# Another order inside a unit of the second attention, parameter rows by GpSimd's queue, the last row tile quantised in halves

## The chip, the cores and the metric

The kernel runs on one core of one Trainium2 chip. The time is the device time of one execution in microseconds (us); of three runs the median is shown. The core has five engines with a queue of instructions each: TensorE (PE in the profile, its weight loads are PEld), VectorE (DVE), ScalarE (ACT), GpSimd (POOL) and SyncE (SP), which here only issues DMAs. Instructions of one engine run in the order of the program; between engines they wait for semaphores.

## The reference

Two transformer blocks, one after the other, over x of 4 batches x 1024 rows x 512 features, with a condition vector of 512 for each batch:

```python
# block 1
tp = gelu(time_emb) @ Wt + bt;  scale, shift = split(tp, 2)
h = layer_norm(x, ln1_g, ln1_b) * (1 + scale) + shift
q, k, v = split_heads(h @ Wqkv)                    # 16 heads of 32
scores = q @ k.T / sqrt(32) - torus_dist * torus_scale   # padded keys to -1e30
x = x + (softmax(scores) @ v) @ Wout
x = x + (gelu(layer_norm(x, ln2_g, ln2_b) @ W1 + b1) @ W2 + b2)
# block 2: bitlinear(x, w, b) = act_quant(x) @ ternary(w).T + b
xn = rmsnorm(x, g1) * (1 + scale1) + shift1        # scale1, shift1 = bitlinear(c, w_ada1)
q, k, v = split_heads(bitlinear(xn, w_qkv, b_qkv))
x = x + bitlinear(softmax(q @ k.T / sqrt(32)) @ v, w_proj, b_proj)
xn = rmsnorm(x, g2) * (1 + scale2) + shift2
x = x + bitlinear(gelu(bitlinear(xn, w_fc1, b_fc1)), w_fc2, b_fc2)   # 2048 hidden
```

`act_quant` rounds each row to integers of -128 to 127 by its largest absolute value.

## The kernel before

The program runs in five stages: the start (some 36 us: parameters, the condition's product with Wt, the norm of the first rows), the first attention, the first feed-forward part (up to about 2398 us), the second attention (2398 to 3640 us), and the last feed-forward part.

**The attention** (`attention`, from line 252) is one function for both blocks. It goes through units. A unit is 128 query rows of one group of four heads: (batch, head group, chunk of 256 queries, which half of the chunk), so there are 128 units, even ones with the first half of a chunk, odd ones with the second. Units are staggered: while the scores of unit i are made, the exponentials of unit i-1 are finished and turned, and the products of an older chunk are made. Each unit has two halves, c = 0 and 1, by the keys 0 to 511 and 512 to 1023. In a half:

- `scores` (L296): four matmuls, one per head, into four PSUM banks.
- `half` (L1364): VectorE reads the scores of each head out of PSUM into `e`, with a running least value (four half reads). `Order.reads` says for each head after how many turns its read is written.
- `turn` (L319, L322): four times per half, one head's exponentials of 512 keys of the unit before are transposed by TensorE in four 128 x 128 pieces into a bank, and copied out to `pt`. `Order.evict` names the copying engine of each turn: A is ScalarE, D is VectorE.
- `weigh` (L480): ScalarE's exponential of one head over 1024 keys; two per half. In half 0 they are those of heads 2 and 3 of the old unit, in half 1 those of heads 0 and 1 of the new one. `Order.exps` says after which turn each is written.
- `product` (L331): in odd units only, the 16 matmuls of each half that multiply `pt` of an older chunk by v; `take` copies the sums out, and `back` (L353, L357) turns them back and scales them, in even units.
- pieces: other work, spread over the slots of the units. A slot is one turn; `Order.even` and `Order.odd` name the slots (0 to 3 in half 0, 4 to 7 in half 1) that take pieces. Here they are the qkv product of the next head group (L1338, L1343, L1346, and its transposes L1354, L1355), quantising and turning the next batch's rows (L197 to L200, L830, L853, L854), and the projection of the batch before (L1282, L1287, L1288). Units that have several kinds of them, as 34 to 39, are called heavy here, those with qkv pieces alone, as 42 to 47, quiet.

The order of all this is written out by hand (`manual_schedule`), so the order of each engine's instructions is that of the program text. In the second attention scores, turns and pieces share seven PSUM banks (L1304, tag "mm"); a new tile takes the bank that the program has freed longest ago, and its first matmul waits until that bank's last reader is done.

**The start** (L499 to L622). SP loads the condition c, four row tiles x in one DMA, the second half of Wt, then the other four row tiles; ScalarE's queue loads the first half of Wt and then, in `load_vectors` (L145), six parameter vectors as rows (`vrows`) and `tscale`. ScalarE's gelu of c (L553) follows in its queue. VectorE measures and norms the rows (L559 to L567). TensorE turns the vectors (v_ps, L579), VectorE copies them out as columns (L580). TensorE makes tp4 (L584, 32 matmuls), VectorE copies it (tpr, L589), TensorE turns it (L592), VectorE adds the bias and makes mod_a and mod_b (L596 to L609). With these ScalarE writes hT (L487), which the first qkv matmuls read (L680).

**The end** (L1377 to L1516). The last part goes through 32 row tiles in a pipeline with a step for each tile (L1498): `hidden` (first product, VectorE L1446, gelu L1450), `hidden_quantised` (VectorE finds the largest value, L1455; `factors` makes the scale, L205 to L208; GpSimd scales and rounds in two passes, L1458 and L1460), `hidden_turned` (16 transposes L1469, ScalarE copies L1472), `second` (16 matmuls, L1479), `stored` (VectorE scales and adds the residual, L1488; GpSimd adds the bias b2, L1489; SP writes out, L1490).

Of the kernel before, what the change touches and what calls it, by code (L numbers as in the profile page):

```python
# [30 lines left out]
F32 = mybir.dt.float32  # L31
BF16 = mybir.dt.bfloat16
U8 = mybir.dt.uint8
AF = mybir.ActivationFunctionType
ALU = mybir.AluOpType
AX = mybir.AxisListType
# [3 lines left out]
P = 128  # L40
B, L, D, H, F = 4, 1024, 512, 16, 2048
HD = D // H
KT = D // P
FT = F // P
FH = FT // 2
LT = L // P
NT = B * LT
# [10 lines left out]
MAGIC = 12582912.0  # L58
# [16 lines left out]
    (((0, 0), (0, 1), (1, 0), (1, 1)), ((2, 0), (3, 0), (2, 1), (3, 1))), (0, 0, 0, 0),  # L75
)
ORDER_L1 = Order(
    ("AADA", "AAAD"), ((1, 2), (2, 2)), 0, (1, 0), (2, 3, 4, 7), (2, 3, 6, 7),
    (((0, 0), (0, 1), (1, 0), (1, 1)), ((2, 1), (3, 0), (2, 0), (3, 1))), (0, 0, 0, 2),
)  # L80


def two_blocks(tc: tile.TileContext, a: dict, out: bass.AP):

    nc = tc.nc
    with tc.tile_pool(name="flag", bufs=1) as pool:
        pairs = pool.tile([1, B * L // 2], mybir.dt.uint16, name="pairs")
        nc.sync.dma_start(
            pairs[:, :].bitcast(U8), a["mask"].rearrange("b l -> (b l)").unsqueeze(0)
        )  # L90
        least = pool.tile([1, 1], mybir.dt.int32, name="least")
        nc.vector.tensor_reduce(least, pairs, AX.X, ALU.min)
        whole = nc.values_load(
            least, min_val=0, max_val=ALL_VALID, skip_runtime_bounds_check_because="bytes are 0 or 1"
        )
    with tc.If(whole == ALL_VALID) as cond:
        program(tc, a, out, masked_keys=False)
    with cond.Else():
        program(tc, a, out, masked_keys=True)
# [3 lines left out]
def program(ctx: ExitStack, tc: tile.TileContext, a: dict, out: bass.AP, masked_keys: bool):  # L103
    nc = tc.nc
# [4 lines left out]
    def row(pool, name, parts=P, tag=None):  # L109

        v = a[name]
        t = pool.tile([parts, v.shape[0]], F32, name=f"row_{name}", tag=tag or f"row_{name}")
        nc.scalar.dma_start(t, v.partition_broadcast(parts))
        return t


    ident = const.tile([P, P], F32, name="ident")
# [17 lines left out]
    nv = sum(vectors.values())  # L135
    vrows = const.tile([nv, P], F32, name="vrows")
    vcols = const.tile([P, nv], F32, name="vcols")
    tscale = const.tile([P, H], F32, name="tscale")
    columns, at = [], 0
# [5 lines left out]
    def load_vectors():  # L145
        at = 0
        for name, n in vectors.items():
            nc.scalar.dma_start(vrows[at : at + n, :], a[name].rearrange("(t p) -> t p", p=P))
            at += n
        nc.scalar.dma_start(tscale, a["L0_cond_torus_scale"].partition_broadcast(P))  # L150


    mod_a = const.tile([P, KT, B], F32, name="mod_a")
# [18 lines left out]
    def copy(i, o, x):  # L172

        if i % 2:
            nc.vector.tensor_copy(o, x)
        else:
            nc.scalar.copy(o, x)
# [24 lines left out]
    def factors(small, am, wmean, deq):  # L202

        n = am.shape[0]
        nc.vector.tensor_scalar(am, am, EPS, 1.0 / 127.0, ALU.max, ALU.mult)  # L205
        s = small.tile([n, 1], F32, name="qs")
        nc.vector.reciprocal(s, am)
        nc.vector.tensor_scalar_mul(deq, am, wmean[:n])  # L208
        return s
# [283 lines left out]
    with ExitStack() as st:  # L493
# [15 lines left out]
        small = st.enter_context(tc.tile_pool(name="l0small", bufs=4))  # L509
        ps_s = st.enter_context(tc.tile_pool(name="l0ps_s", bufs=4, space=PSUM))  # L510
        ps_mm = st.enter_context(tc.tile_pool(name="l0ps_mm", bufs=3, space=PSUM))
# [4 lines left out]
        with tc.tile_pool(name="mod", bufs=1) as ap, tc.manual_schedule(engines=ALL):  # L516
# [6 lines left out]
            xs = [x0[:, t, :] for t in range(4)]  # L523
# [12 lines left out]
            load_wt(nc.scalar, 0)  # L536
            load_wt(nc.sync, 1)
            load_vectors()
            xs += [load_x(0, t) for t in range(4, LT)]

# [31 lines left out]
            def rows_normed(c):  # L572
                for t in range(4 * c, 4 * c + 4):
                    measure(t)
                normed(range(4 * c, 4 * c + 4))

            rows_normed(0)
            v_ps = ps_mm.tile([P, nv], F32, name="v_ps", tag="mm")
            nc.tensor.transpose(v_ps, vrows, ident[:nv, :nv])  # L579
            nc.vector.tensor_copy(vcols, v_ps)  # L580
            tp4 = ps_mm.tile([P, TQ], F32, name="tp4", tag="mm")
            for k in range(KT):
                for j in range(4):
# [2 lines left out]
                        rhs=wt[:, k, bass.ts(j, TQ)], start=(k == 0), stop=(k == KT - 1),  # L586
                    )
            tpr = ap.tile([P, TQ], F32, name="tpr")
            nc.vector.tensor_copy(tpr, tp4)  # L589
            tp_ps = ps_mm.tile([P, TQ // P, 4, 32], F32, name="tp_ps", tag="mm")  # L590
            for n in range(TQ // P):
                nc.tensor.transpose(  # L592
# [231 lines left out]
    means = {n: w1p.tile([P, 1], F32, name=f"mean_{n}") for n in ("q", "p", "a1", "a2", 1, 2)}  # L824
# [68 lines left out]
    with ExitStack() as st:  # L893
# [11 lines left out]
        small = st.enter_context(tc.tile_pool(name="f0small", bufs=2))  # L905
        ps_mm = st.enter_context(tc.tile_pool(name="f0ps", bufs=2, space=PSUM))
        ps_p = st.enter_context(tc.tile_pool(name="f0ps_p", bufs=2, space=PSUM))
        b2r = row(wp, "L0_cond_b2")
# [154 lines left out]
        def part(name, bufs=2):  # L1063
            return cp.tile([P, 2, TC], F32, name=name, bufs=bufs)
# [63 lines left out]
        def block(xs, moving, steps, more):  # L1128
# [31 lines left out]
            a_lo, a_hi = xs[0][:, :, :TC], xs[0][:, :, TC:]  # L1160
            b_lo, b_hi = xs[1][:, :, :TC], xs[1][:, :, TC:]
            p = second(1, "x")
            s = part("s", 1)
            nc.scalar.copy(s, p)
            nc.gpsimd.tensor_tensor(a_lo, a_lo, s, ALU.add)
            p = second(2, "y")
            nc.vector.tensor_tensor(a_lo, p, a_lo, ALU.add)
            p = second(6, "w")
            u = part("y")
            nc.vector.tensor_tensor(u, p, s, ALU.add)  # L1170
# [77 lines left out]
    small = st.enter_context(tc.tile_pool(name="a1small", bufs=4))  # L1248
# [4 lines left out]
    def row_scale3(b, n):  # L1253

        at = slice(b * LT, (b + n) * LT)
        nc.scalar.activation(rms3[:, at], squares[:, at], AF.Sqrt, bias=eps_rms, scale=1.0 / D)
        nc.vector.reciprocal(rms3[:, at], rms3[:, at])
# [40 lines left out]
    with ExitStack() as inner:  # L1298
# [5 lines left out]
        ps_mm = inner.enter_context(tc.tile_pool(name="a1ps_mm", bufs=7, space=PSUM))  # L1304
# [77 lines left out]
    with ExitStack() as inner:  # L1382
        wp = inner.enter_context(tc.tile_pool(name="f1w", bufs=1))
        b1r = row(wp, "L1_cond_b_fc1")
        b2r = row(wp, "L1_cond_b_fc2")
        magic = wp.tile([P, 1], F32, name="magic")
        nc.gpsimd.memset(magic, MAGIC)
        small = inner.enter_context(tc.tile_pool(name="f1small", bufs=6))
# [5 lines left out]
        fp = inner.enter_context(tc.tile_pool(name="f1t", bufs=3))  # L1394
        xfp = inner.enter_context(tc.tile_pool(name="f1x", bufs=LT + 2))
        rows, xs, xns, xqs, xqTs, hs, hqs, hqTs, outs = {}, {}, {}, {}, {}, {}, {}, {}, {}
        HALF = F // 2
# [54 lines left out]
        def hidden_quantised(t):  # L1452
# [7 lines left out]
            nc.gpsimd.tensor_scalar(hq, h, 1.0, -MAGIC, ALU.mult, ALU.add)  # L1460
            hqs[t] = hq, deq

        def hidden_turned(t):
            hq, deq = hqs.pop(t)
            hqT = fp.tile([P, FT, P], BF16, name="hqT")
            for half in range(2):
                tr = ps_tr.tile([P, FT // 2, P], BF16, name="tr_h", tag="tr")
                for k in range(FT // 2):
                    nc.tensor.transpose(  # L1469
                        tr[:, k, :], hq[:, bass.ts(half * (FT // 2) + k, P)], identb  # L1470
                    )
                nc.scalar.copy(hqT[:, bass.ts(half, FT // 2), :], tr)  # L1472
            hqTs[t] = hqT, deq

        def second(t):
            hqT, deq = hqTs.pop(t)
            mm = ps_o.tile([P, D], F32, name="o_ps", tag="o")
            for k in range(FT):
                nc.tensor.matmul(  # L1479
                    mm, lhsT=hqT[:, k, :], rhs=w2[k // KT][:, k % KT, :],  # L1480
                    start=(k == 0), stop=(k == FT - 1),
                )
            outs[t] = mm, deq

        def stored(t):
            mm, deq = outs.pop(t)
            x = xs.pop(t)
            nc.vector.scalar_tensor_tensor(x, mm, deq, x, ALU.mult, ALU.add)  # L1488
            nc.gpsimd.tensor_tensor(x, x, b2r, ALU.add)  # L1489
            nc.sync.dma_start(out[t // LT, bass.ts(t % LT, P), :], x)  # L1490

        left = project(B - 1, o_tiles)
        with tc.manual_schedule(engines=ALL):
            for i in range(-3, NT + 4):
                def step(part, t, *more):
                    if 0 <= t < NT:
                        part(t, *more)

                if i == -2:
                    for k in range(KT):  # L1500
                        nc.sync.dma_start(w2[k], wf2[:, bass.ts(k, KT), :])
                step(stored, i - 3)
                step(hidden_turned, i - 2)
                step(hidden_quantised, i - 1)
                step(hidden, i, 0)
                step(turned, i + 1)
                step(quantised, i + 2)
                step(hidden, i, 1)
                if i >= 0:
                    next(left, None)  # L1510
                if i == 2 * LT:
                    row_scale3(B - 1, 1)
                step(normed, i + 3)
                step(second, i - 2)
# [46 lines left out]
```

## Time and profile before

| what | value |
|---|---|
| median of three runs | 3938.22 us (3936.89 to 3938.29) |
| the profiled execution | 3935.82 us, span 3933.8 us |
| granted TensorE clock, mean | 0.998 |
| PE / PEld busy | 3831.0 (97%) / 2554.3 us (65%) |
| DVE / ACT / POOL busy | 2664.2 (68%) / 2558.9 (65%) / 1351.3 us (34%) |
| second attention, 2398 to 3640 us: PE / DVE / ACT / POOL | 1208.7 / 1026.1 / 1067.6 / 180.1 us |

The profile is of one execution, from the first instruction to the last (the span). In the rows, a time since the span's start is followed by a duration, the engine, the line, the operation, what it writes `<-` what it reads, and how many instructions the row holds (xN). In brackets stands how long the engine was idle before and what ended that. In the rows of groups the part behind the bar is the busy time in us and the mean of one in ns, then the idle time before such instructions and its releasers. The rows of windows give busy time and count of each engine in a stretch, then the granted clock, the share in which DMA engines were busy, and GB/s. An engine with "q" is its queue issuing a DMA.

### The profile page before, as it was taken

To read this page: it belongs to the slowest core of one execution; us is meant where nothing else is said; L and a number is where in the kernel's file an instruction comes from. 1 tells how busy PE (TensorE), PEld (TensorE's weight loads), DVE (VectorE), ACT (ScalarE), POOL (GpSimd) and SP (SyncE) were. 2 spreads that over 40 slices of the span, in tenths; PEclk is the share of its full clock that TensorE was granted. 3 is DMA by queue.
4 is the path that set the end of the run, shared out by engine and by line. 5 is a ranking of instruction groups with operands and counts; after the bars stand their busy time and mean duration, and the time that the engine had idled before them with its cause. 6 is when DMAs were issued, how large, how long until landed. Compare 5 with 4: busy or idle time off the path is not lost. (4 is left out here: it accounts for less than half of the span.)

```text
span 3933.8 us, 78141 instructions
## 1 busy us (share of the span) xinstructions
PE 3831.0 (97%) x29329; PEld 2554.3 (65%) x29379; DVE 2664.2 (68%) x6707; ACT 2558.9 (65%) x4666; POOL 1351.3 (34%) x1464
## 2 busy tenths in 40 slices
PE   8999999999999999999999999999999999999998
PEld 4666666656665665888888886666666666665454
DVE  5666566656664665555565536788888887878897
ACT  5777678757875786222222215888888888888575
POOL 3444344434443442343344430021120110202776
PEclk9999999999999999999999999999999999999999
DMA  4222222222222223676677542000000100101321
GB/s 153 68 82 80 70 90 72 86 79 90 73 87 80 69 65 120 187 234 216 220 256 243 180 142 70 4 26 15 31 28 2 44 20 9 44 2 64 117 73 44
DMA packets 208125, 357.62 MB, mean 91 GB/s; under 512 B 20133, under 2 KB 87245, under 8 KB 207610
## 3 DMA queue, kind: packets, MB, share of 16 engines
q1 hardware_dynamic: 206474, 348.78, 27.7%
q8 instruction: 234, 3.83, 0.4%
q10 hardware_dynamic: 1264, 3.75, 0.3%
q14 instruction: 153, 1.25, 0.1%
HBM read 303.14 MB, written 49.32 MB: 90 GB/s over the span
## 5 line engine op out<-in xcount | busy, mean ns | idle before, releaser
L319 PEld LDWEIGHTS tr<-ident,e 128*128 128x128 f32 x8192 | 899.4, 141 | 551.9 <-issue 168.1
L322 ACT COPY pt<-tr 128x512 f32<-128x512 f32 x1664 | 913.3, 594 | 470.6 <-PE tr L319 468.3
L480 ACT ACTIVATE e<-e,low 128x1024 f32<-128x1024 f32 x1024 | 1183.9, 1164 | 2.1 <-DVE low L728 1.0
L319 PE MATMUL tr<-ident,e 128*128 128x128 f32 x8192 | 1122.7, 278 | 37.6 <-ACT e L480 19.3
L721 POOL TENSOR_SCALAR e<-dist,tscale 128x1024 f32<-128x1024 f32 x512 | 571.6, 1122 | 877.3 <-PE tr L319 763.0
L728 DVE CUSTOM_DVE_ANT_0 e<-scores,e,low 128x512 f32<-128x512 f32 x512 | 353.6, 746 | 318.1 <-PE scores L296 318.1
L331 PE MATMUL acc<-pt,v 128*32 128x256 f32 x8192 | 495.6, 382 | 0.0
L331 PEld LDWEIGHTS acc<-pt,v 128*32 128x32 f32 x8192 | 240.5, 110 | 250.6 <-issue 99.3
L1364 DVE TENSOR_SCALAR_CACHE_REDUCE e<-scores,low 128x512 f32<-128x512 f32 x512 | 359.8, 740 | 57.7 <-PE scores L296 55.9
L728 DVE CUSTOM_DVE_ANT_0 e<-scores,e 128x512 f32<-128x512 f32 x512 | 323.1, 687 | 91.7 <-PE scores L296 91.6
L322 DVE COPY pt<-tr 128x512 f32<-128x512 f32 x384 | 264.2, 688 | 146.8 <-PE tr L319 145.4
L1364 DVE TENSOR_SCALAR_CACHE_REDUCE e<-scores 128x512 f32<-128x512 f32 x512 | 322.7, 686 | 24.9 <-PE scores L296 24.5
L296 PE MATMUL scores<-qkT 32*128 32x512 f32 x2048 | 330.3, 641 | 3.2 <-DVE xr L1287 1.6
L296 PE MATMUL scores<-kT,qT 32*128 32x512 f32 x2048 | 309.8, 640 | 0.8 <-DVE kT L693 0.8
L1346 POOL COPY v<-qk 128x128 f32<-128x128 f32 x128 | 38.8, 303 | 639.5 <-DVE qk L1343 491.0
L680 PE MATMUL qk_ps<-hT,wqkv 128*128 128x512 f32 x512 | 254.3, 595 | 0.0
L480 ACT ACTIVATION_READ_ACCUMULATOR e<-e,low 128x1 f32 x1024 | 210.4, 206 | 0.0
L1098 ACT ACTIVATE a<-y,vcols 128x256 f32<-128x256 f32 x128 | 65.1, 508 | 194.3 <-DVE y L1114 105.6
L1106 ACT COPY s<-px 128x256 f32<-128x256 f32 x64 | 22.7, 355 | 221.4 <-PE px L1092 186.3
L831 POOL TENSOR_TENSOR xn<-xn,ada 128x512 f32<-128x512 f32 x64 | 81.6, 1275 | 206.5 <-DVE xn L830 206.5
L296 PEld LDWEIGHTS scores<-kT,qT 32*128 32x128 f32 x2048 | 91.1, 183 | 93.0 <-issue 52.8
L296 PEld LDWEIGHTS scores<-qkT 32*128 32x128 f32 x2048 | 99.7, 183 | 73.2 <-issue 24.4
(227 smaller groups left out, 5457.8 us busy)
## 6 DMA issues: line engine op xcount, KB each, us to landing
dist<-n_L_cond_torus_dist_dram SPq DMA_DIRECT2D x128, 512.0 KB
xr<-x SPq DMA_DIRECT2D x136, 256.0 KB
w<-w1s SPq DMA_DIRECT2D x128, 256.0 KB
w2q<-w2s SPq DMA_DIRECT2D x128, 256.0 KB
w2q<-in_L_cond_W_dram SPq DMA_DIRECT2D x96, 256.0 KB
w<-w1s SPq DMA_DIRECT2D x64, 384.0 KB
x_in<-in_x_dram SPq DMA_DIRECT2D x84, 256.0 KB
x<-xr SPq DMA_DIRECT2D x64, 256.0 KB
```

What stands on the lines that cost most here:

```text
L296: nc.tensor.matmul(s[j], lhsT=qT[rows, bass.ts(qt, P)], rhs=kT[rows, bass.ts(c, 512)], start=True, stop=mask[b] is None,)
L319: nc.tensor.transpose(tr[:, k, :], es[u, j][:, bass.ts(h2 * (LT // 2) + k, P)], ident)
L322: engine(pt[b, hg, qc, j, h2][:, :, bass.ts(qi, P)], tr)
L331: nc.tensor.matmul(acc[j * HD : (j + 1) * HD, :], lhsT=v[:, k, j * HD : (j + 1) * HD], rhs=pt[b, hg, qc, j, k // (LT // 2)][:, k % (LT // ...
L480: nc.scalar.activation(e, e, AF.Exp, bias=low, scale=-1.0, accum_out=total)
L680: nc.tensor.matmul(mm, lhsT=wqkv[:, k, bass.ds(n * D + hg * P, P)], rhs=hT[b][:, k, bass.ts(half, 512)], start=(k == 0), stop=(k == KT - 1),)
L721: nc.gpsimd.tensor_scalar(e, dists[qt], tscale[:, h : h + 1], 1.0, ALU.mult, ALU.mult)
L728: nc.vector.tensor_tensor_reduce(out=e, in0=s, in1=e, op0=ALU.add, op1=ALU.min, scale=1.0, scalar=low[:, 0:1] if c else 3.0e38, accum_out= ...
L831: nc.gpsimd.tensor_tensor(xn, xn, rows[:, 1, :], ALU.add)
L1098: nc.scalar.activation(o, x, AF.Gelu_apprx_tanh, bias=bf1c[:, at : at + 1])
L1346: nc.gpsimd.tensor_copy(v[:, t, :], qk[:, i, 2 * P :])
L1364: nc.vector.tensor_scalar(e[:, bass.ts(c, 512)], s, -SCALE, low[:, 0:1] if c else 3.0e38, ALU.mult, ALU.min, accum_out=low[:, c : c + 1],)
```

## The change

Three parts, in three stages of the program.

1. `ORDER_L1`, the order inside a unit of the second attention: in half 1 the third turn is copied by VectorE instead of ScalarE; in half 0 the exponential of old head 2 is written after the first turn instead of the second; even units take pieces in slots 3, 4 and 7 instead of 2, 3, 4 and 7; the third head's half read is written after the second turn instead of before the first (the fourth's was there already).
2. The start: the six vector rows and `tscale` are loaded by GpSimd's queue; the transpose of the rows and its copy stand behind the tp4 matmuls; the copies of tp4 and of the rows are ScalarE's.
3. The end, for the last row tile alone: its largest value is found in two halves and joined; the two rounding passes are made in halves, the first half by GpSimd, the second by VectorE; the second copy of its transposes is VectorE's; and b2 is added to the residual ahead of the last 16 matmuls instead of behind them.

```diff
 ORDER_L1 = Order(
-    ("AADA", "AAAD"), ((1, 2), (2, 2)), 0, (1, 0), (2, 3, 4, 7), (2, 3, 6, 7),
-    (((0, 0), (0, 1), (1, 0), (1, 1)), ((2, 1), (3, 0), (2, 0), (3, 1))), (0, 0, 0, 2),
+    ("AADA", "AADD"), ((0, 2), (2, 2)), 0, (1, 0), (3, 4, 7), (2, 3, 6, 7),
+    (((0, 0), (0, 1), (1, 0), (1, 1)), ((2, 1), (3, 0), (2, 0), (3, 1))), (0, 0, 2, 2),
 )
...
-            nc.scalar.dma_start(vrows[at : at + n, :], a[name].rearrange("(t p) -> t p", p=P))
+            nc.gpsimd.dma_start(vrows[at : at + n, :], a[name].rearrange("(t p) -> t p", p=P))
             at += n
-        nc.scalar.dma_start(tscale, a["L0_cond_torus_scale"].partition_broadcast(P))
+        nc.gpsimd.dma_start(tscale, a["L0_cond_torus_scale"].partition_broadcast(P))
...
             rows_normed(0)
-            v_ps = ps_mm.tile([P, nv], F32, name="v_ps", tag="mm")
-            nc.tensor.transpose(v_ps, vrows, ident[:nv, :nv])
-            nc.vector.tensor_copy(vcols, v_ps)
             tp4 = ps_mm.tile([P, TQ], F32, name="tp4", tag="mm")
...
             tpr = ap.tile([P, TQ], F32, name="tpr")
-            nc.vector.tensor_copy(tpr, tp4)
+            nc.scalar.copy(tpr, tp4)
+            v_ps = ps_mm.tile([P, nv], F32, name="v_ps", tag="mm")
+            nc.tensor.transpose(v_ps, vrows, ident[:nv, :nv])
+            nc.scalar.copy(vcols, v_ps)
...
+        def last_quantised(t):
+
+            h = hs.pop(t)
+            ams = small.tile([P, 2], F32, name="ams")
+            for half in range(2):
+                nc.vector.tensor_reduce(
+                    ams[:, half : half + 1], h[:, bass.ts(half, HALF)], AX.X, ALU.max,
+                    apply_absolute_value=True,
+                )
+            am = small.tile([P, 1], F32, name="am")
+            nc.vector.tensor_tensor(am, ams[:, 0:1], ams[:, 1:2], ALU.max)
+            deq = small.tile([P, 1], F32, name="deq_h")
+            s = factors(small, am, means[2], deq)
+            hq = fp.tile([P, F], BF16, name="hq")
+            for half, engine in enumerate((nc.gpsimd, nc.vector)):
+                at = bass.ts(half, HALF)
+                engine.tensor_scalar(h[:, at], h[:, at], s, MAGIC, ALU.mult, ALU.add)
+                engine.tensor_scalar(hq[:, at], h[:, at], 1.0, -MAGIC, ALU.mult, ALU.add)
+            hqs[t] = hq, deq
...
-                nc.scalar.copy(hqT[:, bass.ts(half, FT // 2), :], tr)
+                copy(half * (t == NT - 1), hqT[:, bass.ts(half, FT // 2), :], tr)
...
         def second(t):
+            if t == NT - 1:
+                nc.gpsimd.tensor_tensor(xs[t], xs[t], b2r, ALU.add)
...
-            nc.gpsimd.tensor_tensor(x, x, b2r, ALU.add)
+            if t < NT - 1:
+                nc.gpsimd.tensor_tensor(x, x, b2r, ALU.add)
...
-                step(hidden_quantised, i - 1)
+                step(last_quantised if i == NT else hidden_quantised, i - 1)
```

## The prediction

> **What bounds the kernel now.** I first read the page's busy row, then the windows by stage, the groups of the second attention, and the timelines of the three places that the change touches.
>
> ```profile
> PE 3831.0 (97%) x29329; PEld 2554.3 (65%) x29379; DVE 2664.2 (68%) x6707; ACT 2558.9 (65%) x4666; POOL 1351.3 (34%) x1464
> ```
>
> TensorE is busy nearly all of the span, so at first sight only its work counts. The windows show where that holds less. First the whole second attention, then 40 us of its heavy units (34 to 37: projection, quantising and qkv pieces run inside them), 40 us of quiet ones (42 to 45), and the last row tile.
>
> ```profile
> core 0: us, PE busy (x) PEld busy (x) DVE busy (x) ACT busy (x) POOL busy (x), PEclk, DMA share, GB/s
> 2398.00:3640.00 1242.00, 1208.65 (x11328) 769.44 (x11346) 1026.06 (x2895) 1067.63 (x2023) 180.10 (x292) 1.00 0.08 24
> 2720.00:2760.00 40.00, 38.77 (x364) 24.22 (x361) 36.66 (x110) 32.24 (x64) 16.24 (x25) 1.00 0.14 47
> 2800.00:2840.00 40.00, 40.00 (x375) 25.61 (x374) 31.27 (x87) 34.82 (x66) 1.76 (x6) 1.00 0.01 1
> ...
> 3922.00:3928.00 6.00, 4.73 (x16) 1.77 (x16) 0.75 (x1) 1.18 (x2) 0.08 (x1) 0.78 0.15 52
> ```
>
> In the heavy units VectorE is the fullest of the helpers (36.66 of 40 us), in the quiet ones ScalarE (34.82). A busy TensorE includes matmuls that stand waiting for a bank, so "40.00" is not yet its own bound: from one unit's first score matmul to the next the loop takes 9.70 us in the mean, even units 8.23 and odd ones 11.19. An even unit has 5.8 us of TensorE work without pieces (8 score matmuls 2.1, eight turns of 0.44, 0.2 for the turn back); the shortest take 7.4 to 7.6 and ScalarE is busy in all of that. Even units wait for helpers, odd ones hardly.
>
> ```profile
> L480 ACT ACTIVATE e<-e,low 128x1024 f32<-128x1024 f32 x512 | 589.2, 1166 | 1.0 <-DVE e L1364 0.7
> L319 PE MATMUL tr<-ident,e 128*128 128x128 f32 x4084 | 543.6, 278 | 25.4 <-ACT e L480 16.6 <-DVE e L1364 3.5 <-ACT pt L322 1.9
> L322 ACT COPY pt<-tr 128x512 f32<-128x512 f32 x765 | 411.2, 599 | 128.1 <-PE tr L319 127.8
> L322 DVE COPY pt<-tr 128x512 f32<-128x512 f32 x255 | 175.2, 687 | 93.7 <-PE tr L319 93.6
> ```
>
> What TensorE visibly waits for at its turns is ScalarE's exponential (16.6 us). ScalarE copies three times as many turns as VectorE (765 to 255).
>
> **Part 1, the order of the second attention.** The third turn's copy of the second half goes from ScalarE to VectorE: one of eight per unit, 128 in all. ScalarE's copies follow each other at 0.48 us, VectorE's take 0.69. So ScalarE loses 128 x 0.48 = 61 us of 1067.6, VectorE gains 128 x 0.69 = 88 on 1026.1, and becomes the fuller one (1114 against 1006, of 1242). The other edits add no work: the old unit's third exponential goes one copy earlier, the third head's half read goes behind the second turn, and pieces keep out of turn 2 of even units. They change who stands before whom.
>
> What it does is set by banks. All seven mm banks go round in the order in which the program frees them; in an even unit with one piece in its first half, the fourth score matmul of the second half takes the bank of the first half's second turn now (ScalarE's copy, long done), and of its third turn then (VectorE's copy, which stands behind four half reads). That wait can be seen before the change where a unit's pieces happen to shift the banks by one:
>
> ```profile
> 2842.42 1.14 PE L296 MATMUL scores<-qkT 32*128 32x512 f32 x8
> 2846.04 1.88 PE L296 MATMUL scores<-qkT 32*128 32x512 f32 x8
> 2995.55 0.69 DVE L322 COPY pt<-tr 128x512 f32<-128x512 f32 x1
> 2996.13 1.28 PE L296 MATMUL scores<-qkT 32*128 32x512 f32 x8
> ```
>
> Unit 46 (start 2838.67) has no such wait: its scores end at +4.89. Unit 62 (start 2991.94) has it: the copy ends at +4.30 and the scores at +5.47, 1.17 behind. So in a quiet even unit the group ends at about 5.47 instead of 4.89: +0.58. Behind the waiting matmul on TensorE stand the second half's four turns, and for these wait ScalarE's copies; on VectorE the second half's reads wait for the group. The second line is the next unit's group, which before the change waits in the same way (1.88 instead of 1.14) for a half read; with another bank that wait mostly goes, -0.5 in my walk. I walked the classes of one batch of 32 units so:
> - The three even units without a piece in the first half are bound by ScalarE; a copy less is -0.5 each, 0.1 of it given back in the next unit: -1.2.
> - Quiet pairs 42 to 47: +0.58 - 0.5, but not in every unit; +0.25.
> - Heavy units 34 to 39: VectorE is busy 8.5 of 9.1 us in unit 34 and 11.6 of 12.3 in unit 35; 0.69 more reaches its limit. Unit 35's first scores then wait for the last half read of 34: +0.95, in the units behind it +0.35, +0.64, +0.3: +2.2.
> - Units 50 to 55 +0.15, 56 to 61 -0.8, 62 and 63 +0.2.
> Sum: +0.8 per batch; -0.75 in the first (no projection), +0.7 in the last: together about +1.5 us. Each class has an error of about 0.1 us per unit, so 128 units give -15 to +20.
>
> **Part 2, the start.**
>
> ```profile
> 13.91 1.28 ACT L553 ACT_TABLE_LOAD   x1 [13.91 <-DMA x<-in_x_dram]
> 17.00 3.26 PE L584 MATMUL tp<-wt,gT 128*32 128x256 f32 x32
> 17.39 1.91 DVE L567 TENSOR_SCALAR x<-x,mv,rstd 128x512 f32<-128x512 f32 x4
> 22.11 2.11 ACT L487 ACTIVATE hT<-tr_x,mod_b,mod_a 128x512 f32<-128x512 f32 x3 [4.96 <-DVE mod_b L609]
> ...
> 25.79 3.52 DVE L567 TENSOR_SCALAR x_in<-x_in,mv,rstd 128x512 f32<-128x512 f32 x4
> 26.59 4.79 POOL L721 TENSOR_SCALAR e<-dist,tscale 128x1024 f32<-128x1024 f32 x4 [19.91 <-DMA dist<-n_L_cond_torus_dist_dram]
> ```
>
> ScalarE's queue issues seven small DMAs before its gelu. They wait for earlier transfers: the last two issue at 11.20 and 13.52, when the first Wt half (10.89) and x (13.50) have landed. So the gelu starts only at 13.91. Without them it starts when c is there (10.71): gT at 12.3. The first half of the 32 tp matmuls (its Wt half landed 10.89) runs early; the rest starts when Wt's other half lands (16.13) and ends at 16.2 + 1.63 = 17.9, not 20.26. The copy tpr and the transposes follow to 19.3; VectorE ends its norms at 19.3 too, and needs 0.69 for tp and the mods, as before (21.32 to 22.01). hT starts at 20.1: -2.0. VectorE's two copies (0.19, 0.42) were what lay on this path; on ScalarE they lie beside the norms. If the qkv weights still land at 22.3, only -1.2 is left; if the SP loads collide, -0.5. What is behind is TensorE's, so the gain carries.
>
> Against the move speaks the Trainium skill, "DMA: Bandwidth & Descriptors", sections on the software path (SWDGE): about 2.0 us fixed for each DMA from GpSimd. On ScalarE's queue an issue takes 0.26 to 0.56 us. In a row from 6.5 us, six would be there at 6.5 + 12 = 18.5 by the page's price, 10 by the row's; vrows are needed at about 18.7. Either hides, the first by little; tscale (about 20.5) is needed when dist lands, 26.4. No row here shows such a DMA; I take -2.0, with -2.3 and -0.5 as ends.
>
> **Part 3, the end.**
>
> ```profile
> 3916.53 1.97 POOL L1458 TENSOR_SCALAR h<-h,qs 128x2048 f32<-128x2048 f32 x1 [1.40 <-DVE deq_h L208]
> 3918.59 1.90 POOL L1460 TENSOR_SCALAR hq<-h 128x2048 bf16<-128x2048 f32 x1
> 3920.54 1.34 PE L1469 MATMUL tr_h<-identb,hq 128*128 128x128 bf16 x16 [2.38 <-POOL hq L1460]
> 3922.32 4.73 PE L1479 MATMUL o_ps<-e,hqT 128*128 128x512 bf16 x16 [0.44 <-ACT hqT L1472]
> 3927.92 1.26 POOL L1489 TENSOR_TENSOR xr<-xr,row_L_cond_b_fc 128x512 f32<-128x512 f32 x1 [6.20 <-DVE xr L1488]
> ```
>
> From 3916.5 on there is one chain. Two half reduces and their maximum cost +0.2. GpSimd's halves are 0.99 + 0.95. VectorE's, from L567's 0.54 per 512, would be 2 x 1.08. Side by side both would be done after 2.2 us instead of 4.0. The Trainium skill, "SBUF — State Buffer", section "Who interferes with whom", speaks against it: such a VectorE operation and one of GpSimd hold a shared port pair as an exclusive lock, the second fully blocks. Taken in turns that is 1.94 + 2.16 = 4.1 us, and the split gains nothing. The row is milder: the four L567 beside L721 (from 25.79) take 3.52, two of them held up to 1.35 until GpSimd's operation ends, and then needing only 0.28 more. So GpSimd's half, which the first transposes need, is there after 2.1 to 2.5, VectorE's after 3.1, in time for the second eight. I take 2.3: o_ps starts 4.0 - 2.3 - 0.2 = 1.45 earlier. The b2 add (1.26, with its gap 1.34) leaves the end; it lies in GpSimd's idle time (6.20). The clock was 0.78 in this window (the first o_ps matmuls 0.43 apart, against 3.63 for the whole group before it): a shorter pause may spare it or only shift it, -1.1 to +0.6, I take -0.3. Sum -3.1; ends -1.9 and -4.2. The copy of the second eight transposes, now VectorE's, takes the place of ScalarE's second and lies beside the first eight matmuls.
>
> **Sum** against the profiled execution's own 3935.82 (span 3933.8): +1.5 - 2.0 - 3.1 = -3.6, 3932.2. The median of the runs is 2.4 higher (3938.22), so **3934.6 us**.
>
> **The rivals.**
> - A, as summed: the order is neutral. 0.48. Own range 3928 to 3942.
> - B, ScalarE's relief counts: even units are ScalarE's (7.4 of 7.4 us busy), and 16.6 us of turns wait for exponentials that come earlier. Half of 64 even units by 0.48 is -15; with the ends -5, about 3918. Against it: the bank handed on by VectorE's copy. 0.32.
> - C, VectorE becomes the bound, slower: 42 heavy units (in three batches) each longer by 0.61, VectorE's step from copy to next read; +26 - 5 gives 3959, half of it 3946. For it 36.66 of 40; 4 more copies make 39.3. It decides from where VectorE's work passes a unit's length, which unit 35 just doesn't (12.26 of 12.28). 0.17.
> - D, start and end do nothing (transfers later than reckoned, the lock in full): 3938 to 3940. 0.03.
>
> **How the numbers follow.** A measurement can tell about 0.2% (7.9 us). Below 3930.3: B and 0.06 of A, 0.38. Above 3946.1: C, 0.17. Between: 0.45. The range leaves a tenth at each end: into B to 3915, into C to 3950.
>
> **What would show it.** Right: even units with one piece in the first half with scores ending near +5.5 and a wait for VectorE's copy, those without at 6.9; VectorE about 1114 us in the loop; gelu before 12.5, hT near 20.1; o_ps of the last tile near 3921 relative to the same start, nothing of GpSimd behind the last VectorE operation. Wrong: the even mean well below 8.2 (B), heavy units longer by 0.5 (C), or vrows landing behind 18.7.

## The result, and the profile after

| | before | after |
|---|---|---|
| median | 3938.43 us (3936.89 to 3943.14, 6 runs) | 3953.35 us (3952.46 to 3960.96, 6 runs) |
| the profiled execution, span | 3935.82, 3933.8 us | 3952.46, 3950.6 us |

The ratio is 1.0043, with an interval of 1.0033 to 1.0053: 15 us slower. The forecast was 3934.6, and its range ended at 3950.

The busy row of the page after:

```profile
PE 3870.0 (98%) x29329; PEld 2587.6 (65%) x29379; DVE 2745.3 (69%) x6838; ACT 2505.6 (63%) x4539; POOL 1358.7 (34%) x1471
```

VectorE has 81 us more and ScalarE 53 less. In the second attention alone the windows give 77 more and 53 less, where 88 and 61 were forecast. TensorE is 39 us busier with as many matmuls: what it lost is counted as busy time. The windows show where, first the second attention as it lies now, then 5 us of unit 121:

```profile
2399.00:3660.00 1261.00, 1247.75 (x11330) 800.78 (x11349) 1103.19 (x3022) 1014.26 (x1896) 182.20 (x292) 1.00 0.07 23
3585.00:3590.00 5.00, 5.00 (x42) 2.33 (x42) 3.47 (x10) 0.76 (x3) 1.27 (x1) 0.61 0.18 52
```

From the first to the last first-half score matmul the loop took 1225.3 us before and 1244.4 now: +19.0. Ahead of the loop, the first score matmul of the first attention is 0.65 earlier (36.25 to 35.60). Behind it, from the last score matmul of the second attention to the end of the span, it is 300.6 instead of 303.9. Between the attentions (last score matmul of the first to the first of the second) it was 874.6 instead of 873.2. That stretch is the same code in both, and took 871.7 to 880.0 in the profiles of all the kernels below, so single profiles can't be compared by their span. The comparisons below are made inside the second attention.

The groups of the second attention. The score matmuls before:

```profile
L296 PE MATMUL scores<-qkT 32*128 32x512 f32 x2048 | 330.3, 641 | 3.2 <-DVE xr L1287 1.6
```

The turns, their copies and the score matmuls after:

```profile
L319 PE MATMUL tr<-ident,e 128*128 128x128 f32 x4086 | 532.9, 277 | 7.0 <-ACT e L480 3.7 <-ACT pt L322 1.4 <-DVE e L1364 0.2
L322 ACT COPY pt<-tr 128x512 f32<-128x512 f32 x638 | 363.6, 587 | 195.0 <-PE tr L319 193.3
L322 DVE COPY pt<-tr 128x512 f32<-128x512 f32 x382 | 254.1, 686 | 70.2 <-PE tr L319 69.9
L296 PE MATMUL scores<-qkT 32*128 32x512 f32 x2048 | 374.2, 641 | 2.5 <-ACT qkT L1355 1.3 <-DVE xr L1287 1.1
```

The turns' visible wait for exponentials fell from 16.6 to 3.7 us. But the 2048 score matmuls are busy 44 us longer, while the mean of one is 641 ns in both. Four of them run side by side; when one of the four starts late, the group is busy for longer, and TensorE shows no idle time. Which engine the late ones wait for can be read from the semaphore of their weight load. Score matmuls that start more than 0.05 us after the one before them in their group, on VectorE's semaphore, were 62 before, with 36.7 us in sum, and 195 now, with 81.1; on ScalarE's it was 2.6 us and is 2.7. So the wait is in another place: scores stand for a bank that VectorE hasn't read out.

The difference by units (a unit's length is from its first score matmul to the next unit's):

| units | forecast | measured |
|---|---|---|
| 32, 40, 48 (no piece in the first half) | -0.50 each | -0.48, -0.49, -0.48 |
| 42, 46 and 43, 47 | +0.58 and -0.5 | +0.58, +0.58 and -0.45, -0.45 |
| 34 to 39 (heavy) | +2.2 | +2.8 |
| 44 and 45 | in "+0.25" for 42 to 47 | 0.00 and +0.33 |
| 49, behind 48 | 0.1 given back | +0.66 |
| 50 to 55 | +0.15 | +0.93 |
| 56 to 61 | -0.8 | +0.07 |
| batch 32 to 63 | +0.8 | +4.0 |
| 120 to 126 (quantising for the last part) | not walked | +5.1 |

Of the sum +2.6 lie in even units and +16.4 in odd ones.

The start after, from the timeline:

```profile
9.76 0.58 POOL L150 DMA_DIRECT2D tscale<-_L_cond_torus_scale_dram  x1
10.82 1.28 ACT L553 ACT_TABLE_LOAD   x1 [10.82 <-DMA c<-in_condT_dram]
17.26 1.94 PE L581 MATMUL tp<-wt,gT 128*32 128x256 f32 x16 [2.90 <-DMA wt<-in_L_cond_Wt_dram]
21.27 2.96 ACT L487 ACTIVATE hT<-tr_x,mod_b,mod_a 128x512 f32<-128x512 f32 x4 [1.54 <-PE tr_x L486]
```

The gelu is as early as forecast. The second half of Wt is not: the last 16 matmuls begin at 17.26, not 16.2, and hT at 21.27, not 20.1. The five kernels with the new start have their first score matmul of the first attention at 35.5 to 36.2 in their profiles, the twelve with the old one at 35.9 to 37.0 (means 35.8 and 36.3), so the start is worth about half a us. The end after:

```profile
3936.22 0.75 DVE L1479 TENSOR_SCALAR h<-h,qs 128x1024 f32<-128x1024 f32 x1
3936.36 1.60 POOL L1479 TENSOR_SCALAR h<-h,qs 128x1024 f32<-128x1024 f32 x1 [1.66 <-DVE deq_h L208]
3937.01 1.50 DVE L1480 TENSOR_SCALAR hq<-h 128x1024 bf16<-128x1024 f32 x1
3938.04 1.36 POOL L1480 TENSOR_SCALAR hq<-h 128x1024 bf16<-128x1024 f32 x1
3941.24 3.63 PE L1501 MATMUL o_ps<-e,hqT 128*128 128x512 bf16 x16 [0.71 <-ACT hqT L177]
3944.96 0.75 DVE L1510 SCALAR_TENSOR_TENSOR xr<-o_ps,deq_h,xr 128x512 f32<-128x512 f32 x1 [3.70 <-PE o_ps L1501]
```

The two engines take turns: a record here includes the time that its engine is blocked. VectorE's first pass ends at 3936.97. GpSimd's first is issued at 3936.36 and ends at 3937.96, 0.99 after that: 0.99 is half of its old pass. VectorE's second, from 3937.01, ends 0.55 after GpSimd's first, and GpSimd's second ends 0.89 after VectorE's second (half of the old one is 0.95). The matmuls take 3.63 as in the tile before, where the last tile's took 4.73 before the change, and nothing of GpSimd follows VectorE's last operation.

### The profile page after: what moved, and what is told of

Its sections match the earlier page's. It is cut to its first block, busy times and chain, and to the rows that moved or that the text cites. A ratio compares the mean times of both kernels' runs of the same rounds, so it can differ in the third digit from the quotient of the medians.

```text
span 3950.6 us, 77950 instructions
## 1 busy us (share of the span) xinstructions
PE 3870.0 (98%) x29329; PEld 2587.6 (65%) x29379; DVE 2745.3 (69%) x6838; ACT 2505.6 (63%) x4539; POOL 1358.7 (34%) x1471
## 5 line engine op out<-in xcount | busy, mean ns | idle before, releaser
L322 ACT COPY pt<-tr 128x512 f32<-128x512 f32 x1536 | 865.9, 589 | 537.1 <-PE tr L319 533.7
L721 POOL TENSOR_SCALAR e<-dist,tscale 128x1024 f32<-128x1024 f32 x512 | 573.5, 1125 | 871.1 <-PE tr L319 755.9
L322 DVE COPY pt<-tr 128x512 f32<-128x512 f32 x512 | 343.7, 687 | 122.5 <-PE tr L319 122.3
L1364 DVE TENSOR_SCALAR_CACHE_REDUCE e<-scores,low 128x512 f32<-128x512 f32 x512 | 359.8, 741 | 50.4 <-PE scores L296 49.5
L296 PE MATMUL scores<-qkT 32*128 32x512 f32 x2048 | 374.2, 641 | 2.5 <-ACT qkT L1355 1.3
L1364 DVE TENSOR_SCALAR_CACHE_REDUCE e<-scores 128x512 f32<-128x512 f32 x512 | 322.5, 686 | 15.9 <-PE scores L296 15.9
L296 PEld LDWEIGHTS scores<-qkT 32*128 32x128 f32 x2048 | 128.5, 183 | 88.1 <-issue 31.7
```

The lines of the kernel that those rows point to most:

```text
L296: nc.tensor.matmul(s[j], lhsT=qT[rows, bass.ts(qt, P)], rhs=kT[rows, bass.ts(c, 512)], start=True, stop=mask[b] is None,)
L322: engine(pt[b, hg, qc, j, h2][:, :, bass.ts(qi, P)], tr)
L721: nc.gpsimd.tensor_scalar(e, dists[qt], tscale[:, h : h + 1], 1.0, ALU.mult, ALU.mult)
L1364: nc.vector.tensor_scalar(e[:, bass.ts(c, 512)], s, -SCALE, low[:, 0:1] if c else 3.0e38, ALU.mult, ALU.min, accum_out=low[:, c : c + 1],)
```

## The experiments

"Units 8 to 119" is the sum of the differences to the kernel before, in the profile, over these 112 units. The first eight are left out because one or two of them were up to 2 us longer in some executions (one such case lies further in, unit 100 of the last run below). The last seven are given apart: between two executions of the same order (the kernel before, and the run below with its order) units 8 to 119 agree in sum to 0.01 us, unit 121 differs by 2.6.

**Where the loss is: the parts.** The first run has the new start and end with the old `ORDER_L1`, the second the new `ORDER_L1` alone.

> The changed start and end with the old order of the second attention. Theory (the order alone makes it slower, start and end gain what their traces show): start -0.65, end -2.8, so 3938.4 - 3.45 = about 3935.0, ratio 0.9991. Rival (the new start puts something late, which is part of the loss): 3938 or more.

Measured: 3934.83, ratio 0.9993 (0.9986 to 1.0). Units 8 to 119: 0.00.

> The new order of the second attention alone, old start and end. Theory: +19 over the 127 units as in the trace of the changed kernel, unit by unit the same, so about 3957.5, ratio 1.0048. Rival (the loss lies partly between start and attention): +13 to +15, 3952 to 3953.

Measured: 3956.91, ratio 1.0048 (1.003 to 1.0067). Units 8 to 119: +12.7, as in the changed kernel (+12.7), unit for unit the same. The loss is the order's; start and end gain some 3 us, about what their traces show (0.65 and 3.05 in the pair of profiles) and less than the 5.1 of the prediction.

**Copy, or the other edits?**

```diff
-    ("AADA", "AAAD"), ((1, 2), (2, 2)), 0, (1, 0), (2, 3, 4, 7), (2, 3, 6, 7),
+    ("AADA", "AADD"), ((1, 2), (2, 2)), 0, (1, 0), (2, 3, 4, 7), (2, 3, 6, 7),
```

> Only the third turn's copy of the second half goes to VectorE; exponentials, piece slots and half reads as before. VectorE theory (its queue from the even unit's last reads into the odd unit's first reads is the limit, and one more copy of 0.61 stands in it): most of the loss, +12 to +20, 3950 to 3958; odd units longer. Order theory (VectorE could carry the copy, it is the later exponential, slots and third read that put things late): +0 to +4, 3938 to 3942.

Measured: 3940.62, ratio 1.0003 (0.9996 to 1.0009). Units 8 to 119: -0.1; even units of the whole loop -8.0, odd +11.7.

The next keeps `"AAAD"` with the other three edits.

> Exponentials, piece slots and half reads of the new order, but the third turn's copy stays on ScalarE. VectorE theory: -3 to +4, 3935 to 3942. Order theory: +12 to +20, 3950 to 3958. Both can add up to the 19 measured, then each is in between.

Measured: 3940.17, ratio 1.0005 (0.9996 to 1.0014). Units 8 to 119: +0.6. Neither the copy alone nor the other three edits do it, and the two don't add up to the 12.7 either: the edits act on each other.

**Which edit meets the copy?** Three runs take one of the other three edits back from the new order.

> The new order without its late third half read (start and end as before the change). The copy alone cost 3.7 us over the loop and the other three edits 5.2, together 21.0, so 12 us come from a meeting of the copy with one of the three. Read theory (the third read then stands behind the turn back and the pieces, and the two copies that VectorE makes at the unit's end stand behind it, so the odd unit's scores wait for a bank that is freed last): +4 to +10 over the loop, 3942 to 3948; the +0.3 to +0.8 of odd units 37, 45, 53, 55, 57 go. Exponential theory: still +17 to +21, 3955 to 3959.

Measured: 3948.01, ratio 1.0022 (1.0015 to 1.0029). Units 8 to 119: +4.5. The excess goes away in 37 (+0.11) and 45 (0.00), as the read theory had it, but 53, 55 and 57 keep theirs (+0.56, +0.36, +0.33): those were not the read's.

> The new order without its earlier exponential. Exponential theory (the second turn's copy on ScalarE stands behind it and ends at +4.3 like VectorE's, so the second half's scores of an even unit with a piece wait 0.58, and the copy's relief of 0.48 in units 58 and 60 is lost): +4 to +10 over the loop, 3942 to 3948; +0.58 gone in units 42 and 46, -0.48 back in 58 and 60. Read theory: +15 to +20, 3953 to 3958, as the odd units stay long.

Measured: 3943.18, ratio 1.001 (1.0001 to 1.0019). Units 8 to 119: +3.2. 42 and 46 at -0.01, 58 and 60 at -0.49 and -0.48, as the exponential theory had it; 37 and 45 stay at +0.78 and +0.33, as the read theory had it. Both theories hold in part.

> The new order with the even units' piece slots as they were. Read and exponential theories alike: +17 to +21 over the loop, 3955 to 3959. Slot theory (fewer slots pack pieces closer, which is what meets the copy): +4 to +10, 3942 to 3948. Units 120 to 125, where the last batch's rows are quantised, should lose less than the +5 of the new order if slots are their cause.

Measured: 3954.02, ratio 1.0032 (1.002 to 1.0043). Units 8 to 119: +11.9. The slots are not the cause. Unit 121 was +1.5 here instead of +3.7, within what it varies by.

**The copy, by place.** Since the copy alone shortens even units and lengthens odd ones, I tried it in some units alone:

```diff
-                            turn(old, *order.groups[c][k], engines[order.evict[c][k]])
+                            light = order is ORDER_L1 and c == 1 and k == 2 and i % 32 in (0, 8, 26, 28)
+                            turn(old, *order.groups[c][k], engines["D" if light else order.evict[c][k]])
```

> Changed start and end, old order, and the third turn's copy on VectorE only in four units of each batch (units 32, 40, 58 and 60 and those that stand at the same place in the other batches), where the kernel with the copy alone was 0.49 shorter and the unit behind it gave back least. If those units keep their gain: 4 x 0.49 less 0.2 in unit 61, about -1.8 per batch, -6 to -7 over the loop, with start and end about 3928 to 3929. If VectorE's later end is carried into the units behind: -3 to 0, 3932 to 3935.

Measured: 3939.66, ratio 1.0001 (0.9993 to 1.001). A miss: units 32, 40 and 58, which have the copy, are at 0.00, -0.01, 0.00, and 123 and 125, behind two chosen units of the last batch, at +1.54. So what had shortened 32, 40 and 58 in the run with the copy everywhere was not their own copy. There the odd unit ahead of each had it too. The next two runs put it in odd units alone (`i % 2`, with the new start and end) and in even units alone (`i % 2 == 0`, with the old).

> Changed start and end, old order, and the third turn's copy on VectorE in odd units alone. Theory (a unit's relief shows one unit later: the copy at the end of an odd unit is what the next even unit's ScalarE is freed from, the copy at the end of an even unit is what delays VectorE's first reads of the odd unit): even units -8 over the loop as with the copy everywhere, odd units 0 to +2, so the loop -6 to -8 and with start and end 3927 to 3930. Rival (the relief is tied to both): loop -2 to +3, 3933 to 3938.

Measured: 3924.02, ratio 0.9962 (0.9949 to 0.9976). Units 8 to 119: -9.3. Even units 32, 40, 48, 58, 60 at -0.48 or -0.49, odd 35 and 61 at 0.00, 49 at +0.07. The median is below the expectation, by more than the loop explains (the last seven units were at -0.5, where the run with the new start and end had +2.1).

> Start, end and order as before the change, and the third turn's copy on VectorE in even units alone, the mirror of the run before. Theory: even units 0, odd units +10 to +12 (35 by +1.0, 49 by +0.67, 123 and 125 by +1.54), 3948 to 3950. Rival: loop +2 to +4, 3940 to 3942.

Measured: 3950.14, ratio 1.0024 (1.0013 to 1.0035). Units 8 to 119: +7.2; 35 at +0.98, 123 and 125 at +1.54, 49 at only +0.24, even units 0.00 (one, 112, at +0.30). So the same copy is worth -9.3 in odd units and +7.2 in even ones. VectorE's queue shows why. The boundary of units 48 and 49, first with the copy everywhere (the run with the copy alone):

```profile
2869.68 1.28 DVE L322 COPY pt<-tr 128x512 f32<-128x512 f32 x2
...
2870.41 1.02 PEld L331 LDWEIGHTS acc<-pt,v 128*32 128x32 f32 x24 [0.46 <-DVE pt L322]
2870.88 0.68 DVE L1364 TENSOR_SCALAR_CACHE_REDUCE e<-scores 128x512 f32<-128x512 f32 x1
```

then with it in odd units alone (this kernel has one line more, L1365 is L1364 of the others):

```profile
2866.06 0.68 DVE L322 COPY pt<-tr 128x512 f32<-128x512 f32 x1
2866.19 1.45 PEld L331 LDWEIGHTS acc<-pt,v 128*32 128x32 f32 x32 [0.76 <-DVE e L1365]
2866.66 0.68 DVE L1365 TENSOR_SCALAR_CACHE_REDUCE e<-scores 128x512 f32<-128x512 f32 x1
```

Unit 49 starts at 2868.66 in the first and 2865.05 in the second. In the first VectorE makes two copies between the last read of unit 48 and the first of 49, and that read starts 2.22 after the unit's start instead of 1.61: the 0.61 of one copy, in an odd unit that VectorE's reads set. A product's weight load waits for the copy too. At the end of an odd unit the copy costs VectorE nothing that shows, and the next even unit, which ScalarE fills, has one copy less of ScalarE's ahead of it (-0.48).

**The exponential and the read alone.**

> Only the earlier exponential; copies, slots and reads as before the change. Theory (the bank of the second turn comes free at +4.3, as VectorE's does): units 42, 46, 62 +0.58 or +0.44, 43 and 47 -0.5 to -0.7; loop +1 to +6, 3939 to 3944. Rival (an earlier exponential lets the turns start earlier, since they waited 16.6 us for exponentials): -5 to 0, 3933 to 3938.

Measured: 3942.4, ratio 1.0009 (1.0003 to 1.0016). Units 8 to 119: +4.0; 42 and 46 +0.58, 43 -0.53, 47 -0.58, but 62 at +0.01. Unit 46 of this run, which starts at 2841.28:

```profile
2844.81 0.59 ACT L322 COPY pt<-tr 128x512 f32<-128x512 f32 x1
2844.89 0.69 DVE L322 COPY pt<-tr 128x512 f32<-128x512 f32 x1
2845.03 1.72 PE L296 MATMUL scores<-qkT 32*128 32x512 f32 x8
2845.63 0.29 PEld L296 LDWEIGHTS scores<-qkT 32*128 32x128 f32 x2 [0.29 <-DVE pt L322]
```

The scores end at +5.47; without the edit they did at +4.89. ScalarE's second copy, which ended at +2.99 before, now stands behind the exponential and ends at +4.12; VectorE's third ends at +4.30. The fourth score matmul now waits for VectorE's third copy: its weight load (the last row) starts at +4.35 on VectorE's semaphore, where before it started at +3.77 on ScalarE's. So the banks of the two copies have changed places; how the place of the exponential in the program leads to that is not shown. This is the +0.58 of the prediction, and its cause is the exponential, not the copy that went to VectorE.

> Only the third head's half read behind the second turn. Theory (without the copy behind it, VectorE catches up before the odd unit's reads): loop -1 to +3, 3937 to 3941, odd units 37 and 45 by +0.1. Rival (the late read alone puts the odd units late): 37 +0.7, 45 +0.3, loop +8 or more.

Measured: 3929.7, ratio 0.9977 (0.9967 to 0.9988). Both theories wrong: the late read alone is a gain. Units 8 to 119: -7.9; 43 at -0.53, 47 at -0.67, 51 at -0.66, 55 at -0.58. The scores of unit 47 of this run:

```profile
2846.37 1.22 PE L296 MATMUL scores<-qkT 32*128 32x512 f32 x8
```

Before, these scores took 1.88 (the line at 2846.04 in the prediction): the fourth matmul started 0.76 after the first, on VectorE's semaphore, behind unit 46's last half read. Now it starts 0.10 after the first, on ScalarE's. With the third read later in the program the banks pass on in another order, and the fourth matmul gets one that ScalarE has long read out; that it is the bank of ScalarE's third copy is argued from the order of the program.

**Where they meet.** If the late read gains because the third copy is ScalarE's, the copy on VectorE takes that away, but only in even units.

> Changed start and end, VectorE's copy in odd units alone, and the late third half read. Theory (late read and copy meet only in even units, where VectorE's copy is then the last of its queue and the odd unit's fourth score matmul waits for a half read instead of ScalarE's copy): the gains add, loop -8.6 - 6.6 = -15, with start and end 3918 to 3922, ratio 0.9950. Rival (they meet anywhere): loop -8 or less gain, 3924 to 3930.

Measured: 3918.18, ratio 0.9944 (0.993 to 0.9957). Units 8 to 119: -14.7 of the -17.2 that the two would sum to.

> Start, end, exponentials and slots as before the change; VectorE's copy in even units alone, and the late third half read. Theory: no gain of the read is left and odd units are longer, loop +12.4 - 6.6 + 10 = +16, 3953 to 3957; 43 and 47 at -0.1 instead of -0.5 and -0.7, 37 at +0.7. Rival (no meeting): +6, 3944 to 3946.

Measured: 3956.47, ratio 1.0042 (1.0026 to 1.0057). Units 8 to 119: +11.7, where the two would sum to -0.7. 43 and 47 at 0.00 and -0.01, so here not even the small gain of the expectation is left; 37 at +0.78. Unit 47 in it:

```profile
2856.35 1.88 PE L296 MATMUL scores<-qkT 32*128 32x512 f32 x8
2856.97 1.28 DVE L322 COPY pt<-tr 128x512 f32<-128x512 f32 x2
2857.11 0.29 PEld L296 LDWEIGHTS scores<-qkT 32*128 32x128 f32 x2 [0.38 <-DVE e L1365]
```

The same 1.88 as before the change: ScalarE's third copy is now VectorE's, written behind the last read, and the fourth matmul waits for that read again (0.76 after the first, as before the change). The gains of the read alone in 43, 47, 51 and 55 are all gone.

> Only the piece slots of even units. Theory (slots matter in few units): loop -2 to +2, 3936 to 3941. Rival (slots carry the 6 us by which the three edits without the copy exceed the sum of exponential and read): +5 to +7, 3944 to 3946.

Measured: 3938.66, ratio 0.9996 (0.9987 to 1.0004). Units 8 to 119: -1.7. Units 19, 51 and 83 are at -0.98 each, six others at about -0.15, and unit 100 alone at +2.03, where 36 and 68, at the same place in their batches, are at 0.00 and no other run has such a step in 100. I take that for this execution's own; without it the slots are worth -3.7.

So the sum of the four edits by themselves, in us over units 8 to 119, is -0.1 + 4.0 - 7.9 - 1.7 = -5.7 (-7.7 without unit 100), and together they make +12.7. The runs with three edits show where the rest comes from, each sum without unit 100:

| three edits | sum of the single ones | measured together |
|---|---|---|
| copy, read, slots | -11.7 | +3.2 |
| exponential, read, slots | -7.6 | +0.6 |
| copy, exponential, slots | +0.3 | +4.5 |

The read and the copy cost each other some 15 us; the two runs of that pair say the same (12.4 in even units, 2.6 in odd ones). The 8 us of the second row are no new wait. In 43, 47 and the eight units like them the exponential and the read each take away 0.5 to 0.7 of the same wait, and together not much more than one of them (-0.53 and -0.74); in 19, 51 and 83 slots and read do the same, by their numbers (-0.98 and -0.66 apart, -0.66 together). That gives 5.2 and 2.9.

The run with the copy in odd units and the late read, with the new start and end, is faster than both kernels: 3918 us, 0.56% under the one before.

## Why the prediction was wrong

Point by point:

- **Start**: -2.0 forecast, -0.65 measured at the first scores. The gelu, the copies and the parameter rows went as written; the term that was mis-sized is the landing of Wt's second half, 17.2 where I took 16.13 from before (17.2 to 17.8 in all five kernels with the new start). SP's loads issue earlier now: the second four row tiles from 6.63 (10.78 before), the qkv weights from 11.01 (17.70 before). That they collide with Wt is what I had named for the low end; it is argued, no run takes them apart.
- **GpSimd's DMAs** were issued in 0.52 to 0.74 us each in this trace, the last by 10.3 us, nearer to the row of ScalarE's queue than to 2.0 for each in a row. They were in flight together, landing 4.9 to 6.5 us after their issue, so a sum of their times was the wrong price. Nothing waited for them.
- **End**: -3.1 forecast; from the reduce to the end of the last engine's operation it took 15.49 us before (3913.69 to 3929.18) and 12.44 now (3933.27 to 3945.71), -3.05. That the sum came out is luck, the parts were not as forecast. GpSimd's half was ready 3.04 after its first issue, not 2.3, and VectorE's was there before it, so o_ps came 0.66 earlier instead of 1.45. The faster matmuls gave 1.10 (3.63 for 4.73) instead of 0.3, and the b2 add 1.3, as said. The Trainium skill's rule ("SBUF — State Buffer", section "Who interferes with whom"), that one of the two blocks the other fully, fits what is measured here: the passes lie one behind the other, 0.75 + 0.99 + 0.55 + 0.95 = 3.2 with the halves of GpSimd's old passes, and the measured pair took 3.2, in all five kernels with the new end. What made the sum by the rule too high (4.1, no gain) was my price for VectorE, 1.08 per pass from two times 0.54. The row of L567 beside L721 had the better one: a blocked operation needed only 0.28 more once it was free, and two times 0.28 is about the 0.55. What made my choice of 2.3 too low was that I took that row for a milder rule: in turns, GpSimd's second pass has the three others ahead of it.
- **Order**: +1.5 forecast, +19 measured. This is where the prediction failed, in three places of its working. First, "the other edits add no work: ... They change who stands before whom" priced the late third read at nothing of its own; by itself it is the largest of the four edits (-7.9 over units 8 to 119), and beside the copy in even units it loses all of that and more. Second, "a copy less is -0.5 each, 0.1 of it given back in the next unit": the gain was exact, but behind 48 the odd unit gave back 0.66, unit 45 and the units 52 to 55 lost more than I had, and 56 to 61 did not gain. Outside the heavy units I followed ScalarE's relief into the even unit and did not follow VectorE's later end into the odd one; +16.4 of the +19.0 lies in odd units. Third, the last seven units were not walked one by one: +5.1. Unit 121 alone is +3.7 of it, and a part of that varies between executions: with the old order its mean granted clock was 0.89 before (11.01 us) and 0.75 in the run with the new start and end (13.60), and it is 0.77 after (14.71).
- **The +0.58** of unit 46 was right to the hundredth, and so was the bank. Which of the four edits moves the bank I had not said; it is the exponential, and not the copy that heads that part of the prediction.
- **Rival C** had the side right and the mechanism half: VectorE's step of 0.61 does decide, but at the boundary from an even to an odd unit, in quiet units as in heavy ones (the heavy ones, 34 to 39, have +2.8 of their batch's +4.0). With VectorE nearly as full in the run with the copy alone (2738.8 us busy, 2745.3 in the changed kernel) the loop lost almost nothing in units 8 to 119. So the load alone isn't the bound. **Rival B**'s waits did vanish from the turns (16.6 to 3.7 us) and more than that came back in the scores.
- The range ended at 3950; an error of 0.1 us per unit was too small, since I had walked each class of units behind one kind of neighbour only.

Left open: how the order of the program leads to the new order of the banks, of which the traces show only the semaphores; why the copy in odd units and the late read gain 2.6 us less together than apart; and what makes unit 121's clock vary.

## What to carry to other kernels

In a loop whose units overlap, an engine freed in one unit can show in the next, so try such an edit by the parity of the unit before judging it: the same copy gained 9 us in odd units and cost 7 in even ones. Where engines share a ring of banks, moving one reader can move later hand-overs too, so edits in it need not add up: test them in pairs. And look for such waits in how long a group of matmuls that needs banks is busy, with the mean of one beside it, not in idle time alone.

## What the runs showed that was not expected

- VectorE's pass over 128 x 1024 took 0.75 where two rows of 128 x 512 had suggested 1.08, so even in strict turns the two engines needed 3.2 us for what GpSimd alone did in 4.0.
- In all five kernels with the new end TensorE waits 1.72 us ahead of the last tile's transposes, and the o_ps matmuls take 3.63. In the twelve with the old end it waits 2.38, and they take 4.08 to 5.74 in eleven and 3.63 in one. So the longer wait mostly goes with slower matmuls, but not always, and the 1.10 of this pair of profiles is one draw of many.
- The stretch between the two attentions, the same in every kernel here, took 871.7 to 880.0 us in single executions, and unit 121 of the same order differed by 2.6 between two, while the units 8 to 119 repeated to 0.01 in sum.
